# A layer's first three tiles issued in an order of their own, with a second PSUM tile for gathered rows, and part of the attention denominators inverted later

## The chip, the cores and the metric

One core of one Trainium2 chip runs the whole program in one launch. The metric is the device time of one execution in microseconds (us). TensorE (PE) multiplies matrices into PSUM, and PEld is its weight load; VectorE (DVE), ScalarE (ACT) and GpSimd (POOL) work on tiles; SyncE (SP) issues nearly all the DMAs of the stages spoken of here. Each engine takes its own instructions in order and waits on semaphores for those of the others.

## The reference

The input is `x` (8 batches x 2048 nodes x 64 features) with an adjacency `adj` (2048 x 2048). Four graph layers follow each other; each adds its output to `x` and normalises over the features. Layer 1, the one that is changed, is an attention over 64 hyperedges with a mix:

```
h = x @ W                                    # per node
agg = softmax over the nodes of an edge (leaky_relu(h @ a_node)) @ h
beta = sigmoid(h @ a_gn (node)  +  agg @ a_ge (edge))
all_he = elu(beta * h + (1 - beta) * agg)    # per node and edge
se = tanh(elu(agg) @ fcW + fcb) @ av         # per edge
g = sum over the edges of a node: softmax(se) * all_he
industry = (adj / deg) @ (x @ W_ind)
out = softmax-weighted mix of industry and g # scores again by tanh(. @ fcW) @ av
x = layernorm(x + out)
```

The softmax over a node's edges needs, for each node, the sum of exp(se) over its edges: these are the weights' denominators of the title. A node has few edges: the kernel takes three of them per node by gathering rows of `agg` with one-hot matmuls, and the others through one more slot and a small reduction.

## The kernel before

The 2048 nodes are 16 tiles of 128 rows, each with 8 batches x 64 features = 512 columns. Layer 1 is `layer1` in the kernel. It has three parts.

A first part computes the edges' values once: `agg` and its parts `agg1` and `nagg` (lines 582 to 591 and 638), their scores (`sep`, line 615), exp of the scores (`ese`, line 621), `ext` (lines 626 to 628, with the row sums of `he`), and the denominators of all 16 tiles: 16 small matmuls into `dnp` (line 633), a copy by ACT (641), an addition, a maximum and a reciprocal by DVE (642 to 644), which land in `hgr[:, :, 1, :]`. Between these stand matmuls of the product for tile 0's industry, `early[0](n)`, n steps of two matmuls (`ind` at line 1296).

Then come the units. `units(j)` is a generator that computes `g` of tile j, in named steps:

- `sx`: the DMA of `oh` (the one-hot matrices of the tile), four small matmuls of it with `ext` (681), one of `S` with `hgr` (685), and a transpose of `S` (167), all into one PSUM tile; `ST`: an ACT copy (692); `gates`: six small DVE operations (698 to 703); `tau`: three small ACT operations that make `sig` and `rest` (706 to 710).
- `ch0`, `ch1`: POOL makes `d = h * sig` (725), two slots of 512 columns, then one.
- `gp0`, `gp1`: two matmuls each gather rows of `agg1` into the PSUM tile `gp` of two banks (738). There is one such buffer.
- `z0`, `z1`: DVE multiplies `gp` by `rest` (745) and adds it to `d` (748); `exp0`, `exp1`: ACT's exp into `gp` (750); `e0`, `e1`: DVE makes `ez` from both (768), which frees `gp`; `w0`, `w1`: POOL multiplies `ez` by `coef` (770), and in `w0` also adds its two halves into `g` (774).
- `dp`: two matmuls (758, 759); `t3`: eight small ACT operations on their result (763).
- `ga`: POOL adds the third slot to `g` (776); `red`: a matmul of the fourth with `ST` (779); `g`: DVE adds that (781).

The third part is the loop over turns. Turn t issues the steps of several tiles interleaved as the string `turns` lists them: `p`, the product for tile t's industry (32 matmuls with a mask tile `mj` of 1 MB that is loaded by SP; line 1468); `u`, the middle steps of unit t+1; `v`, the first steps of unit t+2; `s`, the last steps of unit t; `m`, `o`, `f`, the mix and the norm of tiles t-1, t-2, t-3 (`trm` is the transpose of g and ind, line 167; `fc` at 838; `dlt` at 803, which frees the accumulator of the product; `df` at 847). Ahead of the loop unit 0 runs alone from `sx` to `w1`, then the first steps of unit 1, and turn 0 follows, in which there is no product to compute any more:

```
            run(unit, 0, first)
            run(unit, 0, second)
            run(unit, 1, first)
            for t in range(NT + 3):
```

What stands ahead of turn 1, in which the first product with 32 matmuls comes, is called the ramp below. All of it lies in `program_order()`: PE, DVE, ACT and POOL run their instructions in the order in which the program issues them. DMAs are not part of it; SP has its queue in the order of the program too, and waits there for buffers.

Of the kernel before, what the change touches and what calls it, by code (L numbers as in the profile page):

```python
# [1 line left out]

# [6 lines left out]
F32 = mybir.dt.float32  # L9
# [53 lines left out]
def kernel(  # L63
# [58 lines left out]
    def b_view(t2):  # L122
        return t2.rearrange("p (b c) -> p b c", b=B)
# [423 lines left out]
    def layer1(  # L547
# [10 lines left out]
        S = l1.tile([P, NT, P], F32, tag="S", name="S")  # L558

# [9 lines left out]
        with tc.tile_pool(name="fa", bufs=2) as fa:  # L569
# [10 lines left out]
            with program_order():  # L580
# [12 lines left out]
                nc.vector.scalar_tensor_tensor(he, he, 1.0, agg, op0=ALU.min, op1=ALU.max)  # L593
                early[0](4)
# [16 lines left out]
                )  # L611
                early[0](2)
# [12 lines left out]
                sums = fa.tile([P, 2, B], F32, tag="sums", name="sums", bufs=1)  # L625
                nc.vector.tensor_reduce(sums[:, 0, :], b_view(he), AX.X, ALU.add)
                nc.vector.tensor_copy(sums[:, 1, :], ese)
                parts(ext, sums)

                early[0](NT)  # L630
                dn = ps_tr.tile([P, NT, 2, B], F32, tag="tr", name="dnp")
                for j in range(NT):
                    nc.tensor.matmul(
                        dn[:, j].rearrange("p k b -> p (k b)"), r_(pT[0:E, j * P:(j + 1) * P]),
                        r_(ese2[0:E].rearrange("p k b -> p (k b)")), start=True, stop=True,
                    )
                full = fa.tile([P, BC], F32, tag="full", name="full", bufs=1)
                nc.vector.tensor_scalar(full, agg, -1.0, None, op0=ALU.mult)
                parts(nagg, full)
                rec = fa.tile([P, NT, B], F32, tag="rec", name="rec", bufs=1)  # L640
                nc.scalar.copy(rec, dn[:, :, 0, :])
                nc.vector.tensor_tensor(rec, rec, dn[:, :, 1, :], ALU.add)
                nc.vector.tensor_scalar(rec, rec, TINY, None, op0=ALU.max)
                nc.vector.reciprocal(hgr[:, :, 1, :], rec)
# [27 lines left out]
        def units(j, dst):  # L672

            oh = l1.tile([P, 4, P], F32, tag="oh", name=f"oh_{j}", bufs=4)
            nc.sync.dma_start(oh, lists["oh"][j // 4][:, j % 4])
            sm = ps_s.tile([P, QW], F32, tag="sm", name=f"sx_{j}")

            for u in range(4):  # L680
                nc.tensor.matmul(
                    sm[:, P + 16 * u:P + 16 * u + 16], r_(oh[:, u, :]), r_(extv),
                    start=True, stop=True,
                )
            nc.tensor.matmul(
                sm[:, P + 64:P + 80], S[:, j, :], hgr[:, j].rearrange("p k b -> p (k b)"),
                start=True, stop=True,
            )
            transpose(sm[:, 0:P], S[:, j, :])
            yield "sx"  # L690
            ST = small("ST", f"ST_{j}", (P, P), 3)
            nc.scalar.copy(ST, sm[:, 0:P])
            yield "ST"
            gate = small("gate", f"gate_{j}", (P, 4, B))
            coef = small("coef", f"coef_{j}", (P, 4, B), 3)
            ex = sm[:, P:P + 80].rearrange("p (u k b) -> p u k b", u=5, k=2)
            for t, k, op in ((gate, 0, ALU.add), (coef, 1, ALU.mult)):
                nc.vector.tensor_tensor(
                    t[:, 0:3, :], ex[:, 0:3, k, :],
                    hgr[:, j, k, :].unsqueeze(1).to_broadcast([P, 3, B]), op,  # L700
                )
                nc.vector.tensor_copy(t[:, 3, :], ex[:, 4, k, :])
                nc.vector.tensor_tensor(t[:, 3, :], ex[:, 3, k, :], t[:, 3, :], op)
            yield "gates"

            nc.scalar.activation(gate, gate, AF.Tanh, scale=0.5)
            sig = small("sig", f"sig_{j}", (P, 4, B))
            nc.scalar.activation(sig, gate, AF.Copy, bias=0.5, scale=0.5)
            rest = small("rest", f"rest_{j}", (P, 4, B))
            nc.scalar.activation(rest, gate, AF.Copy, bias=0.5, scale=-0.5)  # L710
            yield "tau"


            def per_b(t, u, n):
                return (
                    t[:, u:u + n, :].rearrange("p u b -> p (u b)").unsqueeze(2)
                    .to_broadcast([P, n * B, C])
                )

            def by_b(t):  # L720
                return t.rearrange("p u (b c) -> p (u b) c", b=B)

            def gated(d, u, n):

                nc.gpsimd.tensor_tensor(
                    d[:, 0:n].rearrange("p u (b c) -> p u b c", b=B),
                    b_view(h_sb[:, j, :]).unsqueeze(1).to_broadcast([P, n, B, C]),
                    sig[:, u:u + n, :].unsqueeze(3).to_broadcast([P, n, B, C]), ALU.mult,
                )

            w = []
            d = small("d", f"d_{j}_0", (P, 2, BC))
            gated(d, 0, 2)
            yield "ch0"
            for i in range(2):
                gp = ps_g.tile([P, 2, BC], F32, tag="g", name=f"gp_{j}_{i}")
                for u in range(2):
                    nc.tensor.matmul(  # L738
                        gp[:, u, :], r_(oh[:, 2 * i + u, :]), r_(agg1), start=True, stop=True
                    )  # L740
                yield f"gp{i}"
                if i == 1:
                    d = d2
                n = 2 - i
                nc.vector.tensor_tensor(  # L745
                    by_b(gp[:, 0:n]), by_b(gp[:, 0:n]), per_b(rest, 2 * i, n), ALU.mult
                )
                nc.vector.tensor_tensor(d, d, gp, ALU.add)  # L748
                yield f"z{i}"
                nc.scalar.activation(gp, d, AF.Exp, bias=minus1)  # L750
                yield f"exp{i}"
                if i == 0:
                    d2 = small("d", f"d_{j}_1", (P, 2, BC))
                    gated(d2, 2, 1)
                    yield "ch1"

                    dp = ps_m.tile([P, BC], F32, tag="m", name=f"dp_{j}")
                    nc.tensor.matmul(dp, S[:, j, :], h_sb[:, j, :], start=True, stop=False)  # L758
                    nc.tensor.matmul(dp, r_(oh[:, 3, :]), r_(nagg), start=False, stop=True)
                    yield "dp"  # L760
                    for b in range(B):
                        bc = slice(b * C, (b + 1) * C)
                        nc.scalar.activation(
                            d2[:, 1, bc], dp[:, bc], AF.Copy, scale=sig[:, 3, b:b + 1]
                        )
                    yield "t3"
                ez = small("ez", f"ez_{j}_{i}", (P, 2, BC))
                nc.vector.scalar_tensor_tensor(ez, gp, 1.0, d, op0=ALU.min, op1=ALU.max)  # L768
                yield f"e{i}"
                nc.gpsimd.tensor_tensor(by_b(ez), by_b(ez), per_b(coef, 2 * i, 2), ALU.mult)  # L770
                w.append(ez)
                if i == 0:
                    g = row("g", f"g_{j}")
                    nc.gpsimd.tensor_tensor(g, ez[:, 0], ez[:, 1], ALU.add)
                yield f"w{i}"
            nc.gpsimd.tensor_tensor(g, g, w[1][:, 0], ALU.add)
            yield "ga"
            mv = ps_m.tile([P, BC], F32, tag="m", name=f"red_{j}")
            nc.tensor.matmul(mv, ST, w[1][:, 1], start=True, stop=True)  # L779
            yield "red"  # L780
            nc.vector.tensor_tensor(g, g, mv, ALU.add)
            dst[j] = g
            yield "g"
# [109 lines left out]
        def layer2(j):  # L893
# [31 lines left out]
        first = "sx ST gates tau ch0"  # L925
        second = "gp0 z0 exp0 ch1 dp t3 e0 w0 gp1 z1 exp1 e1 w1"
        turns = (
            "q.ind u.gp0 u.z0 q.dlt m.xg m.tr0 v.sx m.sT0 v.ST u.exp0 u.ch1 m.fc0 m.tr1 u.dp "
            "o.mult m.sT1 p.i m.th0 f.rstd u.t3 u.e0 p.i o.r m.fc1 v.gates u.w0 o.s u.gp1 p.i "
            "v.tau p.i m.th1 u.z1 s.ga p.i v.ch0 u.exp1 m.sub u.e1 o.centre s.red u.w1 f.x2 p.i "  # L930
# [5 lines left out]
        def run(who, j, whats):  # L936
            for what in whats.split():
                if 0 <= j < NT:
                    got = next(who[j])
                    assert got == what, (j, got, what)  # L940
                    done.add((what, j))
# [12 lines left out]
        with program_order():  # L954
            run(unit, 0, first)
            run(unit, 0, second)
            run(unit, 1, first)
            for t in range(NT + 3):
# [1247 lines left out]
```

## Time and profile before

| | |
|---|---|
| three runs | 1307.51, 1308.96, 1308.96 us; median 1308.96 |
| the profiled execution | 1308.88 us, of which the span from the first to the last instruction is 1307.5 us |
| mean granted PE clock | 0.971 of full |
| PE busy | 1250.4 us, 96% of the span |
| DVE, ACT, POOL busy | 887.6, 378.0, 512.2 us |
| end of the first part of layer 1 (start of `dnp`) | 717.82 us in the span |
| turn 1's first product matmul (`ind`, line 1468) | 758.53 us |
| start of turn 2 and of turn 3 (first `gp` of their units) | 770.27 and 786.42 us |

All times within the span are of that one execution. A line of the timeline gives start, duration, engine, line, operation, what is written and read, shape and count, and in brackets how long the engine had been idle and for whom it waited. A line of waits gives the engine and instruction that waited, for whom, the sum in us, how often, and the longest. A line of windows gives for a stretch of time the busy us of each engine with its instructions in brackets, then the granted PE clock and the DMA's share.

### The profile page before, as it was taken

How to read it: one execution, taken by the hardware profiler on the slowest of the kernel's cores; microseconds unless marked ns; L12 is line 12 of the kernel's file. 1: busy time of each engine (PE TensorE's matmuls, PEld its weight loads, DVE VectorE, ACT ScalarE, POOL GpSimd, SP SyncE). 2: the span in 40 equal slices, each digit the busy share in tenths (PEclk: the TensorE clock that was granted, in tenths of full speed). 3: DMA queues.
4: the chain of work that ended last, by engine and by line, in shares of the span. 5: the costliest groups of instructions: out<-in, count | busy, mean ns of one | idle time of the engine just before them, and what ended most of it. 6: DMA issues, size and time to landing. Idle time of an engine off the chain costs nothing. (4 is left out here: it accounts for less than half of the span.)

```text
span 1307.5 us, 20046 instructions
## 1 busy us (share of the span) xinstructions
PE 1250.4 (96%) x7724; PEld 1005.3 (77%) x7724; DVE 887.6 (68%) x1597; ACT 378.0 (29%) x852; POOL 512.2 (39%) x419
## 2 busy tenths in 40 slices
PE   9999789999999999999998599999998899999996
PEld 8887568888888888888886377777766788888885
DVE  5555368888887777778674567777774666655544
ACT  3000101222222222222222356666665521111111
POOL 1000354555555555555411568888872600000000
PEclk9999889999999999999998599999998999999998
DMA  8889532333332333332352212222220233334551
GB/s 285 253 234 182 162 116 93 108 104 103 107 102 97 108 108 108 108 108 81 121 179 97 80 65 97 97 98 97 81 97 1 82 112 129 107 119 153 184 177 67
DMA packets 100951, 157.22 MB, mean 120 GB/s; under 512 B 12912, under 2 KB 64496, under 8 KB 94832
## 3 DMA queue, kind: packets, MB, share of 16 engines
q1 hardware_dynamic: 98368, 151.65, 35.7%
q10 hardware_dynamic: 2304, 4.20, 0.8%
q8 instruction: 63, 1.03, 0.3%
q0 software_dynamic: 176, 0.02, 0.1%
q14 instruction: 40, 0.33, 0.1%
HBM read 118.08 MB, written 37.76 MB: 119 GB/s over the span
## 5 line engine op out<-in xcount | busy, mean ns | idle before, releaser
L1141 DVE SCALAR_TENSOR_TENSOR r<-pp,emb_sb,r 128x256 f32<-128x256 f32 x512 | 247.3, 483 | 109.1 <-PE pp L1130 94.0
L1130 PE MATMUL pp<-w_sb,xT 64*128 64x256 f32 x1024 | 161.6, 392 | 6.5 <-DVE r L1141 6.5
L1130 PE MATMUL pp<-w_sb,y1T 64*128 64x256 f32 x1024 | 154.1, 377 | 0.0
L1130 PE MATMUL pp<-w_sb,y2T 64*128 64x256 f32 x1024 | 154.1, 377 | 0.0
L1079 POOL TENSOR_TENSOR r<-xs,bn 128x256 f32<-128x256 f32 x32 | 22.8, 732 | 244.6 <-issue 216.8
L1130 PEld LDWEIGHTS pp<-w_sb,xT 64*128 64x128 f32 x1024 | 95.0, 187 | 24.6 <-issue 9.6
L1130 PEld LDWEIGHTS pp<-w_sb,y1T 64*128 64x128 f32 x1024 | 100.3, 188 | 11.0
L1130 PEld LDWEIGHTS pp<-w_sb,y2T 64*128 64x128 f32 x1024 | 100.1, 188 | 10.9
L1093 PE MATMUL y2p<-y_hi,msk 128*128 128x512 f32 x256 | 103.7, 405 | 0.0
L523 PE MATMUL y1p<-x_hi,m 128*128 128x512 f32 x256 | 103.0, 402 | 0.1
L1093 PE MATMUL y2p<-y_lo,msk 128*128 128x512 f32 x256 | 101.9, 398 | 0.0
L1468 PE MATMUL ind<-y_hi,mj_l 128*128 128x512 f32 x240 | 101.7, 424 | 0.0
L523 PE MATMUL y1p<-x_lo,m 128*128 128x512 f32 x256 | 101.0, 395 | 0.0
L1468 PE MATMUL a<-v_hi,mj_l 128*128 128x512 f32 x256 | 100.1, 392 | 0.0
L1468 PE MATMUL a<-v_lo,mj_l 128*128 128x512 f32 x256 | 100.0, 391 | 0.0
L1468 PE MATMUL a<-y_lo,mj_l 128*128 128x512 f32 x240 | 95.1, 396 | 0.0
L1468 PE MATMUL a<-y_hi,mj_l 128*128 128x512 f32 x240 | 94.9, 395 | 0.0
L1468 PE MATMUL ind<-y_lo,mj_l 128*128 128x512 f32 x240 | 94.6, 394 | 0.0
L1032 POOL TENSOR_TENSOR ms<-msk,srow 128x1024 f32<-128x1024 f32 x32 | 90.3, 2821 | 10.0 <-DVE ms L1048 5.7
L770 POOL TENSOR_TENSOR ez<-ez,coef 128x1024 f32<-128x1024 f32 x32 | 69.9, 2184 | 56.2 <-DVE ez L768 54.3
L440 DVE TENSOR_SCALAR msk<-adj 128x1024 fp32r<-128x1024 f32 x32 | 61.9, 1971 | 1.1 <-DMA adj<-in_at 1.1
L745 DVE TENSOR_TENSOR gp<-gp,rest 128x1024 f32<-128x1024 f32 (+1 forms) x32 | 30.9, 966 | 45.3 <-PE gp L738 45.0
(289 smaller groups left out, 2455.5 us busy)
## 6 DMA issues: line engine op xcount, KB each, us to landing
mj_l<-mask SPq DMA_DIRECT2D x46, 1024.0 KB, 4.9
adj<-in_at SPq DMA_DIRECT2D x64, 256.0 KB, 3.9
mask<-msk SPq DMA_DIRECT2D x32, 512.0 KB, 4.6
raw<-in_at SPq DMA_DIRECT2D x31, 512.0 KB, 5.2
oh<-oh SPq DMA_DIRECT2D x32, 128.0 KB, 3.9
xT<-in_xt SPq DMA_DIRECT2D x16, 256.0 KB, 3.0
xs<-in_xn SPq DMA_DIRECT2D x16, 256.0 KB, 2.9
kept<-x SPq DMA_DIRECT2D x16, 256.0 KB, 2.0
```

Source lines behind the costliest of these rows:

```text
L440: nc.vector.tensor_scalar(r_(m), raw, 0.0, None, op0=ALU.is_gt)
L523: nc.tensor.matmul(accs[q][jj], r_(m[:, t, jj * P:(jj + 1) * P]), r_(part[:, mt, :]), start=i + h + t == 0 and part is x_hi, stop=i == 3 a ...
L745: nc.vector.tensor_tensor(by_b(gp[:, 0:n]), by_b(gp[:, 0:n]), per_b(rest, 2 * i, n), ALU.mult)
L770: nc.gpsimd.tensor_tensor(by_b(ez), by_b(ez), per_b(coef, 2 * i, 2), ALU.mult)
L1032: nc.gpsimd.tensor_tensor(ms, m, srow[j].unsqueeze(1).to_broadcast([P, 8, P]), ALU.mult)
L1079: nc.gpsimd.tensor_tensor(r[:, 4 * bq * C:4 * (bq + 1) * C] .rearrange("p (h l c) -> p h l c", h=2, l=2), swapped(terms[j]["xs"], bq), bn. ...
L1093: nc.tensor.matmul(acc, r_(msk[j, mt // 8][:, mt % 8, :]), r_(part[:, mt, :]), start=mt == 0 and part is y_hi, stop=mt == NT - 1 and part ...
L1130: nc.tensor.matmul(pp[:, h, pl, :], terms[j][name][rs, 2 * bq + pl], w_sb[rs, k, dq * 4 * C:(dq + 1) * 4 * C], start=k == 0, stop=k == K - 1,)
L1141: nc.vector.scalar_tensor_tensor(rb, ppv[:, :, dd, :], emb_sb[:, j, d:d + 1], rb, op0=ALU.mult, op1=ALU.add)
L1468: nc.tensor.matmul(acc, r_(a[:, mt, :]), r_(part[:, mt, :]), start=mt == 0 and part is hi, stop=mt == NT - 1 and part is lo,)
```

## The change

It touches the first part and the ramp of layer 1; the turns from turn 1 on keep their order.

1. The denominators of tiles 0 to 3 (`NE = 4`) get a PSUM tile, an ACT copy and the three DVE operations of their own, on 4 x 8 columns. Those of tiles 4 to 15 go by 12 matmuls into a second PSUM tile, an ACT copy into `rest_sums` (a buffer of `own`, tag `b0_11`, which in the kernel before takes a mask part of layer 2 that is loaded early), and DVE's addition, maximum and reciprocal come after unit 1's last step of the ramp.
2. The row sums of `he` and `nagg` with its parts are computed ahead of the wait for the scores. The last step of tile 0's product (two matmuls) moves behind unit 0's `dp`.
3. `units` returns steps that can be called in any order, with `z` split into `m` (the multiplication) and `z` (the addition), and `a0` (the addition of `ez`'s halves) split from `w0`.
4. For tiles 0 and 1 the second gathered pair goes into `ps_fc`, the PSUM buffer that `fc` uses from turn 1 on. For tile 0 the second `d` takes the buffer `pm` of `wts`, and `a0` runs on DVE and not on POOL.
5. The ramp has the order of the string below. Turn 0 is gone, its steps are part of the string.

```diff
+                nc.vector.tensor_reduce(sums[:, 0, :], b_view(he), AX.X, ALU.add)
+                full = fa.tile([P, BC], F32, tag="full", name="full", bufs=1)
+                nc.vector.tensor_scalar(full, agg, -1.0, None, op0=ALU.mult)
+                parts(nagg, full)
                 early[0](2)
...
-                early[0](NT)
-                dn = ps_tr.tile([P, NT, 2, B], F32, tag="tr", name="dnp")
-                for j in range(NT):
...
+                def reciprocals(rec, low, lo, hi):
+                    nc.vector.tensor_tensor(rec, rec, low, ALU.add)
+                    nc.vector.tensor_scalar(rec, rec, TINY, None, op0=ALU.max)
+                    nc.vector.reciprocal(hgr[:, lo:hi, 1, :], rec)
+
+                dn = ps_tr.tile([P, NT, 2, B], F32, tag="tr", name="dnp")
+                weight_sums(dn, 0, NE)
+                nc.vector.tensor_copy(sums[:, 1, :], ese)
+                parts(ext, sums)
+                rec = fa.tile([P, NE, B], F32, tag="rec", name="rec", bufs=1)
+                nc.scalar.copy(rec, dn[:, 0:NE, 0, :])
+                reciprocals(rec, dn[:, 0:NE, 1, :], 0, NE)
+                dn2 = ps_mm.tile([P, NT - NE, 2, B], F32, tag="mm", name="dnp2")
+                weight_sums(dn2, NE, NT)
+                nc.scalar.copy(late[0], dn2)
...
+                pool, tag = (ps_fc, "fc") if ahead and i else (ps_g, "g")
+                gp = pool.tile([P, 2, BC], F32, tag=tag, name=f"gp_{j}_{i}")
...
+            def add0():
+                t["g"] = row("g", f"g_{j}")
+                engine = nc.gpsimd if j else nc.vector
+                engine.tensor_tensor(t["g"], ezs[0][:, 0], ezs[0][:, 1], ALU.add)
...
+        ramp = (
+            "0.sx 0.ST 0.gates 0.tau 0.ch0 0.gp0 0.gp1 0.dp 0.ind 0.ch1 0.m0 0.t3 1.sx 1.ST 0.m1 1.gates "
+            "1.tau 1.ch0 0.z0 0.exp0 0.z1 0.exp1 0.e0 0.w0 1.gp0 1.dp 0.e1 1.gp1 1.ch1 0.w1 "
+            "1.m0 1.z0 1.t3 1.exp0 0.a0 0.ga 1.m1 1.z1 1.exp1 0.red 2.sx 2.ST 1.e0 1.w0 2.gates 2.tau "
+            "2.ch0 0.g 1.e1 1.w1 1.a0"
+        )
...
-            run(unit, 0, first)
-            run(unit, 0, second)
-            run(unit, 1, first)
-            for t in range(NT + 3):
+            for turn_ in ramp.split():
+                j, what = turn_.split(".")
+                if what == "ind":
+                    early[0](NT)
+                    continue
+                run(unit, int(j), what)
+            run(product, 0, "i " * (NT // 2))
+            reciprocals(late[0][:, :, 0, :], late[0][:, :, 1, :], NE, NT)
+            for t in range(1, NT + 3):
```

In the changed program's queues the instructions follow that string; the instructions of the turns from turn 1 on stand in the same order as before. SP's queue has two moves: the mask part of layer 2 that used `b0_11` is now issued after the late reciprocal, and the load of tile 4's `oh` stands ahead of that of `mj` for turn 2. One wait is new by the buffers: the first matmul of unit 0's `sx` waits for ACT's copy into `rest_sums`, since its PSUM tile takes the place of the one that the 12 matmuls wrote. As before there is one PSUM tile for `sx`, so that each unit's `sx` waits for the copy `ST` and the gates of the unit ahead.

## The prediction

> **What bounds the kernel now.** I read the page first, then the windows around the one hole in PE's row, then the waits in it, then PE's timeline.
>
> ```profile
> PE 1250.4 (96%) x7724; PEld 1005.3 (77%) x7724; DVE 887.6 (68%) x1597; ACT 378.0 (29%) x852; POOL 512.2 (39%) x419
> PE   9999789999999999999998599999998899999996
> PEclk9999889999999999999998599999998999999998
> ```
>
> The span is PE's, except in slice 23 (719 to 752 us), where PE is half busy and the clock half granted: the ramp of layer 1. The windows (PE, PEld, DVE, ACT, POOL, then clock, DMA share, GB/s) show that nobody is full there, while in the turns behind it PE is:
>
> ```profile
> 720.00:730.00 10.00, 6.21 (x19) 4.23 (x18) 5.12 (x12) 2.22 (x7) 2.90 (x2) 0.65 0.55 210
> 730.00:740.00 10.00, 5.27 (x19) 4.61 (x20) 6.26 (x11) 3.63 (x15) 5.93 (x4) 0.53 0.08 26
> 740.00:750.00 10.00, 4.92 (x7) 1.53 (x6) 5.61 (x11) 5.27 (x15) 7.11 (x6) 0.50 0.07 26
> 770.00:780.00 10.00, 10.00 (x48) 6.60 (x47) 8.16 (x15) 7.28 (x18) 4.97 (x5) 1.00 0.40 150
> ```
>
> So the ramp is a chain of latencies. The waits between 717 and 758.5 us name it:
>
> ```profile
> PE gp L738 <- DVE ez L768: 13.4, 4, 4.2
> ACT gp L750 <- DVE d L748: 10.9, 4, 3.2
> DVE ez L768 <- ACT gp L750: 5.5, 5, 1.3
> ```
>
> The one `gp` buffer is free only when `ez` has read it; meanwhile DVE waits for ACT's exp and ACT for DVE's `d`. PE's timeline gives the points from which I count:
>
> ```profile
> 717.82 3.55 PE L633 MATMUL dnp<-ese,pT 64*128 64x16 f32 x16
> 721.30 1.02 PE L681 MATMUL sx<-ext,oh 128*128 128x16 f32 x4
> 723.29 0.61 PE L685 MATMUL sx<-hgr,S 128*128 128x16 f32 x2 [0.98 <-DVE hgr L644]
> 750.79 1.19 PE L738 MATMUL gp<-agg,oh 128*128 128x512 f32 x2 [3.07 <-DVE ez L768]
> 751.78 1.05 PE L167 MATMUL trm<-ident,g 128*128 128x128 f32 x4
> 758.53 0.39 PE L1468 MATMUL ind<-y_hi,mj_l 128*128 128x512 f32 x1
> ```
>
> From 758.53 on PE is packed and the turns' order is unchanged, so what the ramp wins or loses up to there goes to the end.
>
> **Part 1, the denominators.** The 16 matmuls start at 717.82 as before: they wait for `ese`'s parts (DVE, 717.55 + 0.17), not for the two `ind` matmuls ahead of them, whose removal (0.96 us) here brings nothing. They take the same 3.55 us, to 721.37. The three DVE operations, 0.29 + 0.23 + 0.95 us on 128 columns, become about 0.20 + 0.18 + 0.36 on 32 (estimate: the small operations' floor of 0.16 and a quarter of the rest) and lie under the other 12 matmuls. The new wait, `sx` for ACT's copy of the 12 tiles (0.27 us for 128 columns, so 0.30 for 192, and 0.2 of hand-overs), starts `sx` at 721.9 instead of 721.30, but then it runs through in the 1.6 us that a later `sx` shows (738.30 to 739.89): the transpose ends at 723.5, not 724.19. Won: 0.7. The late operations on 96 columns cost DVE 1.2 us (0.26 + 0.2 + 0.75) ahead of unit 2's first multiplication. PE's own chain covers them with 1.4 us (below); uncovered they cost 1.2. The reduce, the negation and the parts of `nagg`, 2.2 us, move into the 4.1 us in which DVE waits for `sep`: nothing either way.
>
> **Part 2, unit 0's start.** The gates, `rest` and the first multiplication follow 0.7 earlier (725.0). But PE now issues both gathers (2 x 0.99), `dp` (2.2) and two `ind` (0.93) from 723.4 on, and unit 1's `sx` behind them; `t3` (1.73) stands ahead of unit 1's `ST` on ACT; and DVE has unit 1's gates ahead of unit 0's `z0`. So `t3` runs 727.7 to 729.4, then `ST` 0.3 and the gates 0.8, and `z0` starts at 730.4, or 731.4 if PE's clock stays at half for `ind` and `sx`. Before it started at 727.57. Lost: 2.9 (3.8).
>
> **Part 3, two units interleaved.** From `z0` at 730.4 by durations of the ramp: addition 1.23, exp 1.12, `ez` 1.23, hand-overs 0.2, so POOL's first `w` starts at 734.2; `w0` 1.86, `ch1` 1.0, `w1` 1.90: 738.95. Beside it DVE issues without a hole (each 1.14 apart) both halves of unit 0 and the multiplications of unit 1; PE gathers for unit 1 after the first `ez`, not after both. Then `red` 1.72 to its successor, `sx` of unit 2 1.6, `ST` and gates 1.2, `g` 0.8 with hand-over: tile 0's transpose `trm` starts at 744.3. In the kernel before it starts at 751.78.
>
> One term is missing. For tile 0 the addition of `ez`'s halves moves from POOL (1.27) to DVE, with both inputs in SBUF, just while POOL multiplies in `w1`. The row of that multiplication:
>
> ```profile
> L770 POOL TENSOR_TENSOR ez<-ez,coef x32: 1902/2217/2285, 731.3 to 976.9; 128x1024 f32<-128x1024 f32 x32
> ```
>
> In the ramp it takes 1.90, in the turns up to 2.285, where DVE has more operations with two SBUF inputs. The Trainium skill, page "SBUF — State Buffer", section "Who interferes with whom", speaks against this edit: a DVE instruction with two SBUF inputs contends with a GpSimd one that reads SBUF, and by its lock the other blocks for the whole instruction. By the row `w1` costs 0.38 more, by the rule up to the 0.69 of DVE's addition. I take 0.35, since the row is this very operation: `trm` at 744.65, 7.1 earlier than before.
>
> **Part 4, into turn 1.** From `trm` to the first `ind` PE took 758.53 - 751.78 = 6.75 us before, without a hole and at half clock to the last 0.7 us. After, the same instructions in the same order, so `ind` at 751.4. It must also wait for `dlt`, which frees the accumulator: DVE ends its last `ez` of unit 1 at 745.8, the late reciprocal at 747.0, then 1.14 + 1.23 + 0.1 + 0.75: 750.0, the 1.4 us of cover named above.
>
> What can differ is when the clock comes back. The windows of 1 us show it rise at 727.1, fall at 730.5 and rise again here:
>
> ```profile
> 756.00:757.00 1.00, 1.00 (x6) 0.84 (x5) 1.00 (x3) 0.00 (x0) 0.00 (x0) 0.50 0.22 82
> 757.00:758.00 1.00, 1.00 (x5) 0.53 (x3) 0.64 (x6) 0.69 (x2) 0.85 (x1) 0.59 0.00 0
> 758.00:759.00 1.00, 1.00 (x6) 0.63 (x5) 0.00 (x0) 1.00 (x2) 1.00 (x1) 1.00 0.00 0
> ```
>
> That is 3.7 us after `fc` (754.15) began the dense stretch. Carried over it would rise at 750.7. The Trainium skill, page "TensorE: Matmul & The Clock Gate", Part 1, puts the decision on free-running windows of about 3.4 us, one of them busy: then it may come anywhere from 3.4 to 6.8 us after the stretch begins, up to 3.1 us later than here, in which PE does half the work: up to 1.55 us lost. By the trace alone the sum is 7.1, by the rule's middle about 6.4.
>
> **DMAs.** SP gets no new transfer. The 1 MB mask for turn 1 was issued at 723.30 when the first part's buffers came free; that is now 721.4. It took 5.9 us and is needed at 751. The mask for turn 2 now stands behind tile 4's `oh`, which waits for unit 0's `dp` (727.6): 30 us in hand. The mask part for layer 2 goes out at about 747 instead of before 708, and is read at 1038. Other loads behind it on SP (`xr` of tile 2) wait for POOL anyway. So nothing, and under 0.3 us if one were late.
>
> **Sum.** Unit 0's `z0` starts 2.8 later, the 0.7 won at the start included; from `z0` to `trm` it was 24.2 us and will be 14.25, 9.9 won: 7.1 at `trm`. Less 0.6, the middle of the clock's term: 6.5. The profiled execution is its span of 1307.5 and 1.38 around it, 1308.88, which is 0.08 under the median: 1308.9 - 6.5 = 1302.4 us. As a check: PE's idle in the ramp was 13.4 + 1.0; the new order leaves holes of about 5 (first `ez`), 0.7 (`red`) and 1.1 (`trm`): 7.6 less.
>
> **The rivals.**
> 1. The clock comes back late and PE's chain stays at half clock in unit 1's `sx` too: 1.55 + 1.0 lost against 7.1, and 0.7 more if the addition blocks `w1` fully: 1304.5 to 1305.5. For it: the clock was at 0.50 from 731 to 757. Against: a dense stretch brought it back twice (727.1, 757.8). 0.13.
> 2. Unit 1's gathers, `dp` and `red` (734 to 741) or `trm` and `fc` (744 to 747.6) count as a busy stretch and turn 1 begins at full clock: up to 2.3 us more, then `dlt` bounds: 1300.0. Against: at 744.8 to 747.7 PE was busy and the clock stayed. 0.09.
> 3. Something absorbs it behind the ramp: no change, 1308.9. Against: PE 10.00 of 10.00 in the turns, nothing with a fixed time. That the order isn't what it says falls here; the queues say it is. 0.07.
> 4. Slower: POOL becomes the bound. `w0`, `ch1`, `w1` (4.8 us) stand ahead of `red`, behind which PE holds `sx` of unit 2 and the rest. If DVE, now dense beside POOL, blocked it so that its operations took twice as long, `trm` would come 4.8 later, and turn 1's `red` some 5 more through `w0`, `a0`, `ga`, `w1` of units 1 and 2: 1312. It decides from a loss of 6.5 + 2.6 us. Against: with DVE at 8 to 9 tenths in the turns the operation grew by 0.38, not by 1.9. 0.05.
>
> **The numbers.** The main case, 1300.8 to 1304, has 0.66. The range that leaves 2 in 10 out takes it and most of rivals 1 and 2: 1299.8 to 1305.5, with about 0.7 us of scatter that the three runs show. A change under 0.2% (2.6 us) can hardly be told from none here. Faster: 0.66 + 0.09 + nearly all of 0.13; same 0.07; slower 0.05.
>
> **What would show it.** In the changed profile: `sx` through without the wait for `hgr`; `z0` of unit 0 at 730 to 731.5; waits of `gp` for `ez` down from 13.4 to about 5; `red` at about 739; `trm` at 744 to 746; first `ind` at 751 to 753; turn 2 at 763 to 765 (770.27 before); the shift the same at the end. I am wrong if `z0` comes after 733, if POOL's `w1` in the ramp takes over 2.6, if DVE's late reciprocal stands ahead of the first `ind` in the chain, or if the clock is at half beyond 755.

## The result and the profile after

The changed kernel takes 1302.44 us (median, 1300.81 to 1306.06), the kernel before in the same session 1308.31 (1307.16 to 1311.25): a ratio of 0.9953, with a 95% interval of 0.9942 to 0.9964. The predicted time was 1302.4. A second session gave 1300.9 us, ratio 0.9942 (0.9928 to 0.9955). The profiled execution took 1302.44 us, with a span of 1300.7.

The page of after has PE 4 us less busy, and in slice 23 the hole is shallower: 7 tenths busy at a clock of 6 tenths, where 5 and 5 stood:

```profile
PE 1246.4 (96%) x7724; PEld 1002.3 (77%) x7724; DVE 891.8 (69%) x1601; ACT 378.0 (29%) x853; POOL 512.1 (39%) x418
PE   9999789999999999999998799999998899999996
PEclk9999889999999999999999699999998999999998
```

The windows of after (PE, PEld, DVE, ACT, POOL, then clock, DMA share, GB/s) cover the ramp and a turn:

```profile
720.00:730.00 10.00, 7.28 (x24) 5.29 (x24) 4.37 (x15) 3.65 (x17) 3.70 (x3) 0.66 0.58 196
730.00:740.00 10.00, 6.03 (x16) 3.35 (x16) 9.46 (x10) 5.05 (x12) 7.14 (x5) 0.66 0.17 66
740.00:750.00 10.00, 8.34 (x24) 4.79 (x24) 9.45 (x15) 3.27 (x8) 8.93 (x6) 0.52 0.11 28
770.00:780.00 10.00, 10.00 (x57) 8.26 (x55) 6.90 (x9) 4.36 (x10) 9.58 (x8) 1.00 0.09 28
```

DVE, 5 to 6 of 10 us busy there before, is now at 9.5 from 730 on: the chain that alternated between engines has become a nearly full DVE queue (part of that is DVE waiting for POOL inside its operations, see below). The waits of the ramp (717 to 753 us; in total, times, longest) say the same. PE's wait for the gather buffer is halved (13.4 before), and a short one for `dlt` is new:

```profile
PE gp L759 <- DVE ez L789: 6.8, 2, 5.0
ACT gp L773 <- DVE d L770: 6.5, 3, 4.4
PEld ind L1520 <- DVE dlt L843: 1.4, 1, 1.4
```

PE's timeline of after, at the points from which the prediction counted:

```profile
718.18 1.92 PE L636 MATMUL dnp<-ese,pT 64*128 64x16 f32 x16 [0.95 <-PE sep L623]
720.51 1.02 PE L694 MATMUL sx<-ext,oh 128*128 128x16 f32 x4 [0.41 <-ACT rest_sums L656]
732.65 1.19 PE L759 MATMUL gp<-agg,oh 128*128 128x512 f32 x2 [4.96 <-DVE ez L789]
737.40 1.12 PE L808 MATMUL red<-ez,ST 128*128 128x512 f32 x2 [0.57 <-POOL ez L794]
742.85 1.09 PE L168 MATMUL trm<-ident,g 128*128 128x128 f32 x4 [0.53 <-DVE g L811]
750.73 0.50 PE L1520 MATMUL ind<-y_hi,mj_l 128*128 128x512 f32 x1 [0.21 <-DVE dlt L843]
762.55 0.64 PE L759 MATMUL gp<-agg,oh 128*128 128x512 f32 x2
```

Turn 2's gather is at 762.55 instead of 770.27. What lies ahead of `dnp` moves from one execution to the next by more than most of the effects below (`dnp` starts at 716.8 to 721.1 us in the kernels of this study), so I count from the start of `dnp`. There the gather comes 44.37 us after it instead of 52.45: 8.1 won. The first matmul of layer 2's product (`a`, line 1520) comes 313.24 after it instead of 320.73: 7.5. The 0.6 between is lost at the tail of layer 1: its last gather is still 8.1 earlier, but then the clock is at half for 10.2 us (from 993.1), where before it was for 6.8 (from 1003.6). Of the rest 0.4 lies ahead of `dnp` and 0.3 behind layer 2's start: 6.8 us of span.

### The profile page after: what moved, and what is told of

Same layout as the page of the kernel before. It is cut to its first block, busy times and chain, and to the rows that moved or that the text cites. A ratio compares the mean times of both kernels' runs of the same rounds, so it can differ in the third digit from the quotient of the medians.

```text
span 1300.7 us, 20049 instructions
## 1 busy us (share of the span) xinstructions
PE 1246.4 (96%) x7724; PEld 1002.3 (77%) x7724; DVE 891.8 (69%) x1601; ACT 378.0 (29%) x853; POOL 512.1 (39%) x418
## 5 line engine op out<-in xcount | busy, mean ns | idle before, releaser
L1145 PEld LDWEIGHTS y2p<-y_hi,msk 128*128 128x128 f32 x256 | 48.9, 191 | 13.0 <-issue 1.0
```

The source lines that it names most:

```text
L1145: nc.tensor.matmul(acc, r_(msk[j, mt // 8][:, mt % 8, :]), r_(part[:, mt, :]), start=mt == 0 and part is y_hi, stop=mt == NT - 1 and part ...
```

## The experiments

Distances are in us from the start of `dnp` in the profiled execution, to the first `trm`, to turn 2's gather and to layer 2's product; the ratio is to the kernel before in the same session. Where two intervals overlap, the time does not tell the two kernels apart.

| kernel | `dnp` takes | `trm` | turn 2's gather | layer 2 | ratio (95%) |
|---|---|---|---|---|---|
| before | 3.55 | 33.96 | 52.45 | 320.73 | 1 |
| changed | 1.92 | 24.67 | 44.37 | 313.24 | 0.9953 (0.9942 to 0.9964) |
| changed, again | 1.92 | 24.66 | 44.44 | 313.33 | 0.9942 (0.9928 to 0.9955) |
| ramp alone | 1.92 | 25.33 | 44.42 | 313.27 | 0.9955 (0.9943 to 0.9967) |
| denominators alone | 3.55 | 32.89 | 51.82 | 320.65 | 1.0011 (1.0001 to 1.0022) |
| buffer alone | 3.55 | 31.34 | 49.47 | 317.77 | 0.9991 (0.9981 to 1.0001) |
| reciprocals in the hole | 1.93 | 24.66 | 44.04 | 312.98 | 0.9954 (0.9940 to 0.9967) |
| pair ahead | 1.92 | 24.67 | 44.45 | 313.35 | 0.9950 (0.9932 to 0.9967) |
| `a0` on POOL | 2.00 | 23.98 | 43.94 | 312.92 | 0.9953 (0.9938 to 0.9968) |
| 4 steps in the ramp | 1.92 | 24.69 | 40.38 | 309.64 | 0.9935 (0.9919 to 0.9950) |
| 8 steps | 3.55 | 25.55 | 39.67 | 312.56 | 0.9937 (0.9920 to 0.9954) |
| held, 6 steps | 1.92 | 24.72 | 37.80 | 307.60 | 0.9917 (0.9898 to 0.9936) |
| held, 5 steps | 1.92 | 24.59 | 37.65 | 308.93 | 0.9922 (0.9906 to 0.9938) |
| held, 4 steps | 1.92 | 24.59 | 38.64 | 307.02 | 0.9915 (0.9896 to 0.9933) |

### Which part makes the gain

**The ramp alone.** The changed kernel with all denominators ahead:

```diff
-                weight_sums(dn, 0, NE)
+                weight_sums(dn, 0, NT)
...
-                reciprocals(rec, dn[:, 0:NE, 1, :], 0, NE)
+                reciprocals(rec, dn[:, :, 1, :], 0, NT)
...
-            reciprocals(late[0][:, :, 0, :], late[0][:, :, 1, :], NE, NT)
```

> The new order of the ramp with its second gather buffer and the early DVE moves, but all 16 tiles' denominators copied and inverted ahead, so that no late reciprocals stand at the ramp's end. If the interleaving with the second buffer is the gain (my theory): the transpose of `sx` ends about 1 us later than in the changed kernel (it waits for `hgr` again), `trm` about 0.5 to 1 later; but DVE is without the 3.8 us of late reciprocals, so `dlt` isn't late and the first `ind` starts straight behind `dp`. Turn 2's gather starts at 763 to 764 (before 770.3, changed 762.6), time about 1302.5 to 1303.5. If the split of the denominators makes the gain (rival): nearly all of it is gone, turn 2 at 769 to 770, time 1308. If the granted clock makes part of it (rival): the 16 matmuls of `dnp` again lie in the same stretch of full clock, and turn 2 moves by up to 1.5 either way.

PE's timeline shows `sx` waiting for `hgr` as in the kernel before:

```profile
723.97 0.61 PE L694 MATMUL sx<-hgr,S 128*128 128x16 f32 x2 [0.97 <-DVE hgr L644]
745.45 1.09 PE L168 MATMUL trm<-ident,g 128*128 128x128 f32 x4 [0.53 <-DVE g L807]
```

`trm` comes 0.66 later than in the changed kernel, and turn 2's gather 0.05: of what the split wins at the start next to nothing is left at the end, since from `trm` to `ind` it takes 7.36 here and 7.88 in the changed kernel. The order with its buffer carries the whole gain. (The early DVE moves of point 2 are in this kernel too, but also in the next, where hardly anything is won.)

**The denominators alone**, under the old order with one buffer (besides this diff, `a0` of tile 0 is on POOL and the early product's last pair stands ahead of `dnp`, both as before):

```diff
-            "0.sx 0.ST 0.gates 0.tau 0.ch0 0.gp0 0.gp1 0.dp 0.ind 0.ch1 0.m0 0.t3 1.sx 1.ST 0.m1 1.gates "
...
+            "0.sx 0.ST 0.gates 0.tau 0.ch0 0.gp0 0.m0 0.z0 0.exp0 0.ch1 0.dp 0.t3 0.e0 0.w0 0.a0 "
+            "0.gp1 0.m1 0.z1 0.exp1 0.e1 0.w1 1.sx 1.ST 1.gates 1.tau 1.ch0 "
...
-            ahead = j < 2
+            ahead = False
```

> The changed kernel's denominators alone (4 ahead, 12 inverted at the ramp's end) under the ramp's old order, with one gather buffer and tile 0's first sum on POOL. If the interleaving is the gain (my theory): the start gains about 0.7 to 1 us at the transpose of `sx`, and the late reciprocals (3.8 us of DVE beside POOL in the changed kernel) lie between the last `z1` or `e1` and `dlt`, so that they take back 0 to 3 us: turn 2 at 768 to 771 (before 770.3), time 1307 to 1310. If the split is the gain (rival): turn 2 at 763 to 765, time 1302 to 1304.

The waits of the ramp have PE waiting for the buffer as long as before:

```profile
PE gp L760 <- DVE ez L790: 13.4, 4, 4.2
```

`trm` 1.1 earlier, turn 2 0.6, layer 2 0.1: nothing is left. The time is 0.01 to 0.22% above before. No stretch from `dnp` to layer 2 shows that; in the profiled execution 1.7 us lie ahead of `dnp` and 1.3 behind layer 2's start, and why is open.

**The buffer alone**, as the one edit to the kernel before:

```diff
-                gp = ps_g.tile([P, 2, BC], F32, tag="g", name=f"gp_{j}_{i}")
+                pool, tag = (ps_fc, "fc") if j < 2 and i else (ps_g, "g")
+                gp = pool.tile([P, 2, BC], F32, tag=tag, name=f"gp_{j}_{i}")
```

> The kernel before with one edit: tiles 0 and 1 put their second pair of gathered rows into the PSUM buffer of `fc`. If the order is needed (my theory): the gather of the second pair no longer waits for `ez` (1.4 us each for two tiles), but DVE's and POOL's order stays, so part of it is kept: `trm` 2 to 3 us earlier than before's 751.78, turn 2 at 766 to 768, time 1304.5 to 1306. If the buffer makes the whole gain (rival): turn 2 at 763, time 1302.4. If the chain through POOL hides the wait for the buffer (second rival): turn 2 at 770, time 1308.

The ramp's waits: most of that for `ez` is gone, but PE now waits for `g` instead:

```profile
PE trm L167 <- DVE g L782: 5.1, 1, 5.1
PE gp L739 <- DVE ez L769: 4.4, 2, 3.0
```

Turn 2's gather is 3.0 earlier: three eighths of the 8.1. The time didn't follow as forecast: its interval takes in no change at all. The rest needs the order: with the old one DVE still runs `z`, exp, `ez` of one half before it starts the next. The order without the second buffer can't be run, so its share alone isn't known: in DVE's queue `0.m1`, which reads the second pair, stands ahead of `0.e0`, which would have to free the only buffer for that pair.

### The steps that were mis-sized

**The late reciprocals in DVE's hole** (they go behind tile 0's second `m`, about 725 us):

```diff
-            ... 1.sx 1.ST 0.m1 1.gates "
+            ... 1.sx 1.ST 0.m1 0.rs 1.gates "
...
-            reciprocals(late[0][:, :, 0, :], late[0][:, :, 1, :], NE, NT)
```

> The changed kernel with the 12 late reciprocals moved from the ramp's end to DVE's idle stretch behind tile 0's second `m` (about 726 us), where POOL is idle too. If DVE's lateness is nearly covered by PE (my theory): the three operations take about 0.3, 0.2 and 0.8 us there (1.2 to 1.19, 1.79 and 0.76 at the ramp's end beside POOL), `dlt` is ready 3 us earlier, and the first `ind` starts only 0.2 earlier, straight behind `dp`, since PE is the bound: time within 0.5 of the changed kernel's. If the late reciprocals are a real cost (rival): the first `ind` comes 2 to 3 us earlier, time 1299 to 1300.

At the ramp's end, first DVE's timeline of after, then POOL's with the operations that run there:

```profile
743.76 1.19 DVE L643 TENSOR_TENSOR rest_sums<-rest_sums 128x96 f32<-128x96 f32 x1
744.98 1.79 DVE L644 TENSOR_SCALAR rest_sums<-rest_sums 128x96 f32<-128x96 f32 x1
746.80 0.76 DVE L645 RECIPROCAL hgr<-rest_sums 128x96 f32<-128x96 f32 x1
749.93 0.74 DVE L843 SCALAR_TENSOR_TENSOR dlt<-ind,sdeg,g 128x512 f32<-128x512 f32 x1
```

```profile
742.93 1.91 POOL L748 TENSOR_TENSOR d<-h,sig 128x1024 f32<-128x1024 f32 x1
744.79 1.92 POOL L794 TENSOR_TENSOR ez<-ez,coef 128x1024 f32<-128x1024 f32 x1
```

In the hole, DVE's timeline of this kernel:

```profile
725.45 0.25 DVE L643 TENSOR_TENSOR rest_sums<-rest_sums 128x96 f32<-128x96 f32 x1
725.73 0.93 DVE L644 TENSOR_SCALAR rest_sums<-rest_sums 128x96 f32<-128x96 f32 x1
726.70 0.75 DVE L645 RECIPROCAL hgr<-rest_sums 128x96 f32<-128x96 f32 x1
```

The addition ends with POOL's `d` (744.84) and the maximum with POOL's `ez` (746.71), within about 0.1 us: each waited out the rest of a POOL operation that had begun before it, while POOL's own took 1.9 as ever. In the hole the addition began as one POOL operation ended (725.53) and took 0.25; only the maximum waited (0.93, to 726.66; POOL's ends at 726.59). `dlt` is done at 746.9 instead of 750.7, and still the first `ind` comes only 0.4 earlier, straight behind `dp`; the time does not move. PE covers the late reciprocals all but 0.4 us.

**`a0` of tile 0 on POOL**

```diff
-                engine = nc.gpsimd if j else nc.vector
+                engine = nc.gpsimd
```

> The changed kernel with tile 0's first sum (`a0`) on POOL instead of DVE. On DVE it took 1.54 us, ending with POOL's `w1`; on POOL it should take 1.27 ahead of `ga`, which waited 0.69 for DVE. If the sum is off the critical chain (my theory): DVE is 1.5 us earlier at `m1`, POOL's `ga` about 0.6 later, and turn 2 stays within 0.3 of 44.4 us after the start of `dnp`: time within 0.5 of the changed kernel's. If the move to DVE carries a part of the gain (rival): `trm` about 0.6 to 1.3 later, time 1303 to 1304. If it costs (second rival): `trm` up to 1.5 earlier, time 1301.

In after, DVE's `a0` was held up until POOL's `w1` ended at 737.34, and was done 0.55 later (DVE's timeline of after, then POOL's); here POOL has it as a step of 1.27 (POOL's timeline of this kernel):

```profile
736.35 1.54 DVE L801 TENSOR_TENSOR g<-ez 128x512 f32<-128x512 f32 x1
```

```profile
735.44 1.90 POOL L794 TENSOR_TENSOR ez<-ez,coef 128x1024 f32<-128x1024 f32 x1
```

```profile
736.38 1.27 POOL L801 TENSOR_TENSOR g<-ez 128x512 f32<-128x512 f32 x1
```

`trm` comes 0.7 earlier and turn 2's gather 0.4: the move to DVE costs a little in the ramp rather than winning. In the time it can't be seen.

**The early product's last pair ahead of `dnp`.** In the changed kernel the clock was full until 720.0 and `dnp` took 1.92 us; before, it fell at 716.9 and `dnp` took 3.55. The first six kernels split by whether that pair stood ahead of `dnp`, so I took its place for the cause:

```diff
+                early[0](NT)
                 dn = ps_tr.tile([P, NT, 2, B], F32, tag="tr", name="dnp")
```

> The changed kernel with one edit: the early product's last pair of matmuls stands ahead of `dnp` again, as in the kernel before. In the three kernels that have it there the 16 matmuls of `dnp` took 3.55 us at half the granted clock, in the three that have it later 1.92 to 1.93 us at full. If its place decides that (my theory): `dnp` takes 3.55 us here too, `sx` and all behind it come 1.0 to 1.6 us later, and turn 2's gather stands 45.4 to 46.0 us after the start of `dnp` (44.4 in the changed kernel, 52.5 before): time 1303.5 to 1304.5. If the ramp's order decides it (rival): `dnp` takes 1.9 us, turn 2 at 44.4, time 1302.5 to 1303.

My theory fell. PE's timeline has `dnp` at full clock with the pair ahead, and the kernel with 8 steps in the ramp (below), which is the changed kernel up to `dnp`, has it at half:

```profile
717.25 1.92 PE L636 MATMUL dnp<-ese,pT 64*128 64x16 f32 x16 [0.39 <-issue]
```

```profile
718.23 3.55 PE L636 MATMUL dnp<-ese,pT 64*128 64x16 f32 x16 [0.95 <-PE sep L623]
```

The code ahead of `dnp` doesn't decide it: executions of the same code there differ. The rival, that the new order of the ramp decides, falls with the second line, since that kernel has the new order too. What does decide it is open. In the four kernels with half clock it falls 0.9 to 1.3 us ahead of `dnp`'s start, in the ten others 1.7 to 2.1 behind it, about one step later of the grid of 3.41 us that is worked out below. That fits a phase of the clock that differs from execution to execution; no run sets this phase. Its worth: `trm` is at 25.55 with 8 steps and at 24.69 with 4, so by this pair some 0.9 of the 8.1 us between the two profiled executions may be the clock's.

### What is left in the ramp

PE is still idle for 5.0 us in the ramp, then for 1.9, while turn 1 behind it is full. Product work of tile 1 can fill it once tile 0's product has left the one accumulator:

```diff
                 if what == "ind":
                     early[0](NT)
+                    run(product, 0, "i " * (NT // 2) + "ind")
                     continue
+                if what == "i":
+                    run(product, 1, "i")
+                    continue
...
+                nc.vector.tensor_tensor(dlt, ind, g_of[j], ALU.subtract)
...
-            "0.sx 0.ST 0.gates 0.tau 0.ch0 0.gp0 0.gp1 0.dp 0.ind 0.ch1 0.m0 0.t3 1.sx 1.ST 0.m1 0.rs 1.gates "
-            "1.tau 1.ch0 0.z0 0.exp0 ...
+            "0.sx 0.ST 0.gates 0.tau 0.ch0 0.gp0 0.gp1 0.ind 0.dp 0.ch1 0.m0 1.sx 1.ST 0.t3 0.m1 0.rs 1.gates "
+            "1.tau 1.ch0 1.i 1.i 1.i 1.i 0.z0 0.exp0 ...
```

> The kernel with the late reciprocals in DVE's hole, and with PE's idle stretch of 5.0 us in the ramp filled with work of turn 1: ACT takes tile 0's product out of PSUM ahead of `t3` (the difference `dlt` of tile 0 is then made from that copy), so that the accumulator is free, and 4 of the 8 steps (16 matmuls) of tile 1's product run behind tile 1's `sx`; turn 1 leaves its first two and its last two steps out. If turn 1 is bound by PE's work and PE's clock falls because PE is idle (my theory): 16 matmuls at 0.23 us leave turn 1 (3.7 us), and `trm` and `dp` run at full clock (another 0 to 1.5): turn 2 at 38.8 to 40.5 us after the start of `dnp` (44.0 with the reciprocals in the hole), time 1297.5 to 1299.5. If turn 1 is bound by the chain through DVE, ACT and POOL (rival): PE waits there instead, turn 2 at 42 to 44, time 1301 to 1303.

Turn 2 at 40.38, 3.7 us earlier than with the reciprocals in the hole, the 16 matmuls' worth and no more. The windows of after, then of this kernel, show why the clock brought nothing: full in the filled stretch, it falls in the next one, where PE waits 2.5 us for POOL ahead of `red` (PE's timeline, third fence).

```profile
737.00:747.00 10.00, 7.20 (x26) 4.40 (x26) 9.42 (x15) 5.09 (x13) 7.55 (x6) 0.67 0.08 28
```

```profile
727.00:737.00 10.00, 6.33 (x26) 4.29 (x25) 9.16 (x13) 7.28 (x23) 6.67 (x4) 0.99 0.54 184
737.00:747.00 10.00, 9.20 (x27) 5.48 (x28) 9.09 (x15) 3.86 (x8) 7.73 (x5) 0.50 0.01 2
```

```profile
736.86 2.07 PE L808 MATMUL red<-ez,ST 128*128 128x512 f32 x2 [2.50 <-POOL ez L794]
```

The median, 1301.1 us, lies above the 1297.5 to 1299.5 expected, and the interval overlaps that of the changed kernel.

All 8 steps in the ramp (`1.i` five times behind `1.ch0`, twice behind `1.gp1`, once behind `2.ch0`; none in turn 1):

> As the kernel with 4 steps of tile 1's product in the ramp, but with all 8 of them there: 5 behind tile 1's `sx`, 2 ahead of `red`, 1 ahead of the next tile's second gather; turn 1 has none. If PE's work bounds turn 1 all the way (my theory's upper end): another 3.7 us, turn 2 at 35 to 37 us after the start of `dnp`, time 1294 to 1296. If the chain takes over on the way (I hold this likelier): turn 2 at 37.5 to 40, time 1296 to 1299, with waits of PE for `ez` and `th` in turn 1. If the matmuls in the ramp delay `gp` and `red` (rival): `trm` 1 to 2 us later, time 1299 to 1302.

Turn 2 at 39.67, but `df` waits for DVE's `th` in a turn 1 that has run out of work, the clock falls at 757.9, and from turn 2 to layer 2 it takes 272.9 us where the one with 4 steps takes 269.3; 3.2 of these 3.6 lie between turn 2's two gathers, where it is at half clock. The chain is the bound there, as I held likelier, but the median of 1301.9 us is above the 1296 to 1299 that I had for that case. PE's timeline:

```profile
756.07 1.97 PE L890 MATMUL df<-av_sb,th 128*128 128x1 f32 x16 [2.42 <-DVE th L886]
```

To keep the clock full with less work taken from turn 1, the next kernels put idle repeats of the product's first matmul ahead of its steps:

```diff
+            for _ in range(8 if j == 1 else 0):
+                nc.tensor.matmul(acc, r_(a[:, 0, :]), r_(i_hi[:, 0, :]), start=True, stop=True)
             for mt in range(NT):
```

With 6 steps (2 behind `1.ch0`, 2 behind `1.gp1`, 1 behind `2.ch0`, 1 ahead of `trm`):

> As the kernel with 4 steps of tile 1's product in the ramp, but spread so that PE's clock should not fall there: behind tile 1's `sx` 8 repeats of the product's first matmul (their result is overwritten; they only keep PE busy) and 2 steps, 2 steps ahead of `red`, 1 behind the next `sx`, 1 between the gather of tile 2 and `trm`; turn 1 keeps 2 steps. If PE's clock between `trm` and turn 1's gather is what is left to win (my theory): the clock stays full from about 727 on, `trm` to turn 1's second gather takes 6 to 7 us instead of 8.9, turn 2's gather comes 37 to 38.5 us after the start of `dnp` (40.4 with 4 steps), time 1298 to 1300. If the chain through the other engines bounds this stretch (rival): PE waits at full clock, turn 2 at 39.5 to 40.5, time 1301. If the added matmuls stand ahead of `gp`, `red` or `trm` (second rival): `trm` over 25.2 us after the start of `dnp`, time above 1301.

With 4 (14 repeats; 1, 2, 1, none ahead of `trm`):

> The same with 14 repeats and 1 step behind tile 1's `sx`, 2 steps ahead of `red`, 1 behind the next `sx`; turn 1 keeps 4 steps, as in the kernel with 4 steps in the ramp. Against that kernel only the clock differs. If the clock holds and matters (my theory): turn 2's gather 38 to 39.5 us after the start of `dnp` (40.4), time 1299 to 1300.5. If the clock falls all the same behind `red` (rival): turn 2 at 40 to 40.6, time 1301.

With 5 (12 repeats; 1, 2, 1, 1), and the changed kernel beside it:

> The two kernels with repeats put together: 12 repeats and 1 step of tile 1's product behind its `sx`, 2 steps ahead of `red`, 1 behind the next `sx`, 1 ahead of `trm` (5 in the ramp); turn 1 keeps 3 steps, one of them behind `dp`, where PE waited 2.1 us for `th` with 2 steps left. If the chain through ACT and DVE bounds turn 1 once PE's clock holds (my theory): turn 2's gather 37.6 to 38.3 us after the start of `dnp` (37.8 with 6 steps, 38.6 with 4), layer 2 starts 306 to 307.6 after it, time 1297.5 to 1299.5. If PE's work still bounds it (rival): 38.3 to 38.7, time as with 4 steps.

> The changed kernel itself once more, beside the fullest version and on the same chip, to set the two side by side and to see how far a second execution of it moves. If the stretch from `dnp` on is fixed but for the clock's phase (my theory): turn 2's gather 44.0 to 45.6 us after the start of `dnp`, `dnp` either 1.9 us at full clock or 3.6 at half; what lies ahead of `dnp` scatters by 1 to 3 us. Time 1301.5 to 1304. If the order fixes the clock too (rival): `dnp` takes 1.92 again.

With 6 and with 5 steps the clock is full from the filled stretch to turn 2; with 4 it is at half once, from 744.2 to 747.6. The windows of the one with 5:

```profile
737.00:747.00 10.00, 8.97 (x45) 5.67 (x43) 8.94 (x15) 4.10 (x9) 7.89 (x5) 1.00 0.01 2
747.00:757.00 10.00, 8.28 (x46) 5.84 (x45) 7.78 (x13) 6.82 (x18) 9.92 (x8) 1.00 0.47 156
```

From `trm` to turn 1's second gather these three take 7.2 us, the kernel with 4 steps and no repeats 8.9. The chain bounds turn 1 from here on: PE waits for `th`,

```profile
748.34 1.13 PE L883 MATMUL fc<-sT,fcw_sb 64*128 64x512 f32 x4 [1.15 <-ACT th L878]
```

and 5 steps reach turn 2 no later than 6. In both the clock then falls for 3.4 us in turn 2, so that the one with 4 steps, 0.8 to 1.0 behind at turn 2, is 0.5 to 0.7 ahead at the layer's last gather. At layer 2 it is 0.6 ahead of 6 steps and 1.9 of 5, which misses the 306 to 307.6 expected: with 5 steps the clock is at half for 10.2 us at the layer's tail, with 4 and 6 for 6.8. All three beat the kernel before (0.9915 to 0.9922), and from `dnp` to layer 2 they take 4.3 to 6.3 us less than the changed one. By time, on the same chip, the kernel with 5 steps is 2.4 us under the changed one (medians 1298.53 and 1300.9), but the intervals overlap (0.9906 to 0.9938 and 0.9928 to 0.9955): the gain over the changed kernel is shown in the profiled executions, not by time. Which of the three is best can't be told.

## Why the prediction was right, and where only its sum was

**The mechanism held.** Two units interleaved with a second gather buffer, read at `trm`: from `z0` to `trm` 14.25 us was predicted and 13.97 measured (728.88 to 742.85), 24.2 before. `z0` in DVE's timeline before and after:

```profile
727.57 1.22 DVE L748 TENSOR_TENSOR d<-d,gp 128x1024 f32<-128x1024 f32 x1 [0.63 <-POOL d L725]
728.88 2.34 DVE L770 TENSOR_TENSOR d<-d,gp 128x1024 f32<-128x1024 f32 x2
```

The waits of `gp` for `ez` were to fall from 13.4 to about 5 in the ramp and fell to 6.8: the one foreseen, 4.96, and 1.88 ahead of `trm`. `trm` to `ind` to turn 2, in the order said, carried it on, and the turns keep the distance until the layer's tail.

**Part 1 was right in size, wrong in what else moved.** `sx`'s transpose was to come 0.7 earlier. It ended 2.3 earlier (4.08 us after `dnp`'s start instead of 6.37), because `dnp` ran at full clock: the step "they take the same 3.55 us" failed. Where it did take 3.55 (8 steps), the transpose ended 5.71 after its start: 0.66 earlier. So the split itself gave the 0.7 foreseen; and ramp alone shows it given back at the other end, which the sum didn't have.

**Part 2, `z0` at 730.4,** came at 728.88, 10.7 us after `dnp`'s start instead of 12.6. Of these 1.9, 1.6 lie at `dnp` and 0.3 in the gathers and `dp` behind it. Had `dnp` run at half clock, not all of the 1.6 would have been missing: with 8 steps, where it did, `z0` came 11.56 after its start, with 4 steps 10.69. The clock was full again 8.9 us after `dnp`'s start in both, so the later chain ran more of its matmuls at full clock. The points behind `z0` came early with it: `z0`, `red` (737.40), `trm` (742.85), the first `ind` (750.73) and turn 2 (762.55) all lie 0.3 to 1.6 us ahead of what was forecast for them.

**The late reciprocals and `a0`: the sign of the contention was wrong.** I had DVE's 1.2 us covered with 1.4 to spare, and POOL's `w1` slowed by 0.35. POOL's `w1` stayed at 1.90; it was DVE that waited: the three reciprocal operations took 3.7 us and not 1.2, and `a0` 1.54. The Trainium skill, page "SBUF — State Buffer", section "Who interferes with whom", has both sides: the shared pair of ports is an exclusive lock, and the order of issue decides who blocks. I read it for one side only. POOL's operations here are up to 1.9 us long and often stand back to back, and DVE's `a0`, the addition and the maximum each came second. One of my conditions for being wrong thereby came true in small: DVE's late reciprocals did stand ahead of the first `ind`, by 0.21 us. The cover had also been summed 0.2 too large: 747.0 and the four terms behind it give 750.2, not 750.0.

**Part 4.** From `trm` to `ind` 7.35 was predicted (6.75 and 0.6 for the clock), and 7.88 measured: `dp` and the `fc` ahead of it at half clock throughout, the clock back only with the first `ind`. The windows of after:

```profile
749.00:750.00 1.00, 1.00 (x3) 0.34 (x1) 1.00 (x2) 0.00 (x0) 1.00 (x2) 0.50 0.63 227
750.00:751.00 1.00, 0.79 (x3) 0.28 (x2) 0.67 (x2) 0.96 (x1) 0.16 (x1) 0.64 0.68 170
751.00:752.00 1.00, 1.00 (x6) 0.80 (x6) 0.73 (x1) 1.00 (x3) 0.00 (x0) 1.00 0.25 94
```

The term was of the right kind and about half a microsecond short (its own middle is 0.7, of which the sum took 0.6). The free-running windows of the Trainium skill, page "TensorE: Matmul & The Clock Gate", Part 1, describe what is seen: in after the clock changes at 720.0, 726.8, 730.2, 737.1, 740.5 and 750.7, within 0.1 us of a grid of 3.41 us.

**The total** agrees to 0.04 us, and that is luck: errors of about 2 us each way cancel. Counted from `dnp`, `trm` came 2.2 us earlier than summed (24.67, not 26.83), 1.6 of it at `dnp`. Against that stand 0.6 more from `trm` to turn 2, 0.6 at layer 1's tail, 0.7 ahead of `dnp` and behind layer 2's start, and 0.4 outside the span (1.7 us, not 1.38): 6.4 between the two profiled executions, where 6.5 was predicted. The kernel before also moved, from the median of 1308.96 that the prediction started from to 1308.31, so that by medians the change is 5.9 us. The rivals: POOL did not become the bound (`red` waits 0.57 for it), nothing was absorbed, turn 1 did not begin at full clock, and the late clock took its toll but with more gain against it.

## What to carry to other kernels

Where a ramp is a chain across engines, a second buffer is worth more with an order that uses it: alone it gave 3.0 of 8.1 us, because the same engines went on waiting for each other in the old order. Work put off from a chain's head must land where its engine is idle and its neighbour on the shared port is too, or it costs that engine twice its time (3.7 us here, 1.9 in the hole). An idle stretch of PE was paid for twice in this ramp, in lost time and in half clock afterwards; matmuls of the next stage can fill it as long as that stage isn't bound by its own chain.

## What had not been expected of the hardware

- Operations of 96 columns on DVE took 1.19 and 1.79 us beside POOL and 0.25 and 0.93 in the hole; each of the long ones ended within about 0.1 us of the end of the POOL operation begun before it, also the maximum with a single SBUF input.
- Counted on its grid of 3.41 us, PE's clock held through a stretch in which PE was idle for 1.2 us (the kernel with 4 steps and no repeats, 729.9 to 733.3) and fell after stretches with 2.0 idle (740.8 to 744.2 with 8 steps) and 2.4 (733.3 to 736.8 with 4): in the first of these two gaps of 1 us were enough.
- Executions of the same code ahead of `dnp` had that stretch at full clock or at half: 1.6 us at `dnp`, some 0.9 at `trm`.
